# An RWKV-style block on one core: one list of pieces in place of ranks and a planner, and three activation table sets instead of two

## The chip, the cores and the metric

The kernel runs on one core of one Trainium2 chip. The metric is the device time in microseconds. TensorE (PE) multiplies matrices, VectorE (DVE), ScalarE (ACT) and GpSimd (POOL) work on elements, and SyncE (SP) issues most of the DMAs; each engine works through its own instructions in their order. Everything is float32.

## The reference, cut to what matters

```python
# x: 8 batches of 256 tokens, 512 channels; 32 heads of 16
xn = ln(x); sx = token_shift(xn) - xn                    # the token before
xxx = tanh((xn + sx * maa_x) @ maa_w1)                   # five groups of 32
x5 = xn + sx * (maa_stack + xxx @ maa_w2)                # five mixed inputs
w = exp(-exp(time_decay + tanh(x5[1] @ decay_w1) @ decay_w2))
r, k, v = x5[3] @ Wr.T, x5[0] @ Wk.T, x5[2] @ Wv.T
g = silu(x5[4] @ Wg.T)
for t in range(256):                                     # a scan over the tokens
    a = k[t] * v[t];  out[t] = r[t] @ (u * a + s);  s = a + w[t] * s
x = x + (groupnorm(out) * gn_w + gn_b) * g @ Wo.T
xn2 = ln(x); xk, xr = xn2 + sx2 * ffn_maa_k, xn2 + sx2 * ffn_maa_r
x = x + sigmoid(xr @ Wr2.T) * (relu(xk @ Wk2.T) ** 2 @ Wv2.T)
```

## The kernel before, in words

The kernel first describes its work as 2679 pieces (`Op`): 394 on PE, 498 on DVE, 1136 on ACT, 379 on POOL and 272 DMAs on SP's queue. A piece is one instruction, or on PE a group of matmuls that go together. Only then are the pieces put in order and emitted; within an engine that order is the order of the instructions.

The pieces come in three stages for each of the 8 batches `b`. `inputs_of_scan` takes the layer norm (`normed`, `ahead`), transposes (`psT`, L633), makes `xin`, multiplies it by `maa_w1` (`psx`), takes the tanh (`ta`), mixes (`psm`, five groups `x5_b_g`, on DVE L803 or L799 and POOL L809), multiplies by the decay weights (`psd`, then the tanh `tb` and `w`) and projects to k, r, v and g (`psk`, `psr`, `psv`, `psg`; L438). `scan` multiplies r by k (`pc`), and for each of four blocks of channels fills `wrep` with the decay on ACT (L955; there is one buffer `wrep`, in PSUM), loads v broadcast over the partitions (`vs`), multiplies by k (DVE L972), scans (DVE L974, into `st8`), multiplies by r (POOL L977) and gathers on PE (`pat`, L985). `rest` takes the group norm (`sq`, `pv`, `rs`; the copies in L1040 spread `rs` over the partitions into `rsb`), multiplies by `Wo` (`pso`), and runs the feed-forward part (`psfk`, `psfr`, `psfv`). PSUM has six buffers `ps` for all of PE's results.

Batch 0 begins with its own input `xt0`, the vectors `vec`, the identity `idt`, and the centering matrix `cen`, by which PE multiplies the raw weights `Wraw0` and `Wraw1` (`psW`). `xw` are four small products of `vec` on DVE (L567) that batch 0's `xin` needs. Twelve matmuls on zeros come ahead of all that.

In the kernel before, each piece has a rank (`TURNS`, a row for each stage). `order` is a planner: it takes the pieces by rank, gives each a start from costs and delays written in the kernel (`LATENCY`, `LANDS`, `TAKES`), gives it a buffer of its pool that is planned to be free (the one freed latest), and sorts by planned start. A matmul also reserves the tile that its result will be copied into (`into`).

A matmul's weights are loaded either as 128 columns or as four tiles of 32 columns; `tiles` chooses per piece by what stands ahead of it on PE.

ScalarE's functions need a table set to be loaded. `Exp` and `Ln` use one set, `Tanh` and `Silu` another; where the next piece needs the other one, a load is emitted (L1132).

Of the kernel before, what the change touches and what calls it, by code (L numbers as in the profile page):

```python
# [12 lines left out]
P = 128  # L13
# [11 lines left out]
TABLES = {"tanh": "silu_and_others", "exp": "natural_log_exp_and_others"}  # L25
# [15 lines left out]
class Buf:  # L41


    def __init__(self, pool, name, view=lambda t: t):
        self.pool, self.name, self.place, self.left, self.view = pool, name, None, 0, view
        self.writers, self.readers, self.until = [], [], 0.0
        self.before, self.since = set(), 0.0
# [15 lines left out]
class Op:  # L63
    def __init__(self, engine, us, outs, ins, emit, mode):
        self.engine, self.us, self.emit, self.mode, self.narrow = engine, us, emit, mode, False
        self.bufs = list(dict.fromkeys([*outs, *ins]))
        self.before, self.after, self.waits = [], [], 0
        self.ready = self.start = self.end = 0.0
        self.number, self.kind = 0, engine + "".join(c for c in self.bufs[0].name if not c.isdigit())


class Plan:
# [4 lines left out]
    LATENCY = {"PE": 0.25, "DVE": 0.13, "ACT": 0.14, "POOL": 0.06, "DMA": 1.65}  # L77
    LANDS = {"vs__": (2.44, 1.6), "s": (0.1, 1.7), "vo_": (0.4, 1.9), "vo__": (0.46, 1.5), "o_": (0.4, 1.6), "ms": (0.15, 2.0), "rb": (0.9, 1.8), "xn__": (0.8, 1.7), "x": (2.3, 1.1), "xt": (1.65, 2.1), "xt_": (0.8, 1.7),
             "Wo_": (1.75, 1.5), "Wfk_": (1.7, 1.5), "Wfr_": (1.75, 1.4), "Wfv_": (1.65, 1.5), "Wg": (1.6, 2.4), "y_": (0.3, 0.6)}
    EARLY = {"xt0_0": (0.76, 1.28), "xt0_1": (0.76, 1.2), "cen": (0.35, 2.1), "vec": (0.2, 2.3), "xt1": (1.4, 2.3), "xt2": (1.4, 2.0), "idt": (0.17, 2.4), "Wfr0_1": (1.4, 1.5),  # L80
             "Wraw0": (1.65, 2.1), "Wraw1": (1.65, 2.0)}
    SWITCH = {"ACT": 1.38, "PE": 0.11}
    AHEAD = {"PE": 0.1}
    GAP = {"PE": 0.0, "DVE": 0.16, "ACT": 0.12, "POOL": 0.12, "DMA": 0.03}

    TAKES = {("ACTsq_", 0.315): 0.415, ("ACTrsb_", 0.315): 0.415, ("ACTpsm__", 0.405): 0.358, ("ACTxn__", 0.495): 0.45, ("ACTw_", 0.405): 0.357,
             ("ACTw_", 0.315): 0.33, ("ACTtb", 0.315): 0.39, ("ACTta", 0.315): 0.28, ("ACTk_", 0.53): 0.48, ("ACTr_", 0.53): 0.48, ("ACTv_", 0.53): 0.485,
             ("ACTg_", 0.53): 0.494, ("ACTo_", 0.53): 0.495, ("ACTxn__", 0.102): 0.085, ("ACTmn_", 0.102): 0.11, ("ACTatt_", 0.394): 0.374, ("ACTvs__", 0.193): 0.19,
             ("ACTvo_", 0.37): 0.4, ("ACTsq_", 0.405): 0.49, ("PEpsm__", 0.875): 0.945, ("PEpsm__", 0.45): 0.52, ("PEpsw_", 0.875): 0.915, ("POOLvs__", 1.959): 2.25}
    LOOSE = ("ACTatt_", "ACTrsb_", "ACTsq_", "ACTxn__", "ACTxk_", "ACTxr_", "ACTxin_", "ACTxh__", "ACTtb", "ACTw_", "ACTold_")  # L90
    SMALL = ("ACTsq_", "ACTrsb_", "ACTatt_")

    def __init__(self):
        self.stages, self.pools, self.bufs = [[]], {}, {}

    def pool(self, name, tiles):
        self.pools[name] = [[0.0, t] for t in tiles]
        self.bufs[name] = []
# [6 lines left out]
    def add(self, engine, us, outs, ins, emit, mode=None, into=(), lag=0.0, kb=0, part=False):  # L105
        outs, ins, into = ([getattr(b, "buf", b) for b in bs] for bs in (outs, ins, into))
        op = Op(engine, us, outs, ins, emit, mode)
        op.lag, op.wire = self.LATENCY[engine] + lag, 0.0
        op.small = 0.12 if op.kind in self.SMALL and round(us, 3) in (0.315, 0.394) else 0.0
        op.shared = engine == "DVE" and (op.kind in ("DVEhm", "DVExk_") or op.bufs[0].name.startswith("x5_0_2") and round(us, 3) == 0.603)  # L110
        op.gap = 0.0 if op.kind in self.LOOSE else self.GAP[engine]
        op.us = self.TAKES.get((op.kind, round(us, 3)), us)
        if kb:
            name = op.bufs[0].name
            op.wire, op.lag = self.EARLY.get(name) or self.LANDS.get("".join(c for c in name if not c.isdigit()), (kb / 370, 2.0))


        op.bufs += [b for b in into if b not in op.bufs]
# [10 lines left out]
        for o in edges - {op}:  # L129
            op.before.append(o)  # L130
            o.after.append(op)
        self.stages[-1].append(op)

    def stage(self):

        self.stages.append([])
        return len(self.stages) - 2


    TURNS = """  # L140
# [236 lines left out]
def tile_rwkv_block(  # L377
# [25 lines left out]
    nc = tc.nc  # L403
# [805 lines left out]
```

## Time and profile before

| | |
|---|---|
| median of 3 runs | 605.47 us (604.45 to 605.61) |
| profiled execution, its span (first to last instruction) | 604.9 us |
| PE busy | 593.1 us (98%) |
| DVE busy | 538.8 us (89%) |
| ACT busy | 516.8 us (85%) |
| POOL busy | 507.9 us (84%) |
| table loads by the planner's order (L1132) | 43, 1283 ns each |
| moved by DMA | 128.07 MB, mean 212 GB/s |

The profiled execution's own time is its span and what lies around it; it isn't listed beside the runs, and the span lies between their lowest and highest time. A line number belongs to the kernel before. Many lines are those of helpers: L438 is every ordinary matmul, L427 every DMA on SP. "Idle before" is the time in which an engine stood still ahead of an instruction, with what ended it.

### The profile page before, as it was taken

The page shows a single profiled execution, that of the slowest core. Times are in us where ns is not written, and L with a number is a line of the kernel's source. Part 1 is how long each engine was busy: PE and PEld are TensorE (multiplying, and loading weights), DVE is VectorE, ACT ScalarE, POOL GpSimd, SP SyncE. Part 2 cuts the span into 40 slices and gives each one's busy share as a digit, 9 for nine tenths or more (in the row PEclk, how much of TensorE's full clock was granted, in tenths as well). Part 3 has the DMA queues.
Part 4 walks back from the last instruction along what each step waited for, and adds up shares of the span by engine and source line. Part 5 has one row for each costly group of instructions (what it writes and reads, how often), then busy time and mean ns, then how long its engine had stood idle before and what let it go on. Part 6 is the DMA issues. An engine that isn't in the chain of part 4 may idle for free.

```text
span 604.9 us, 19630 instructions
## 1 busy us (share of the span) xinstructions
PE 593.1 (98%) x8236; PEld 345.0 (57%) x8236; DVE 538.8 (89%) x500; ACT 516.8 (85%) x1207; POOL 507.9 (84%) x390
## 2 busy tenths in 40 slices
PE   8899999899999999999999999999999999999997
PEld 7675656467438864365553754465654474455464
DVE  5699999999999999998789999999999999994432
ACT  4898989999999999988999898999999889964531
POOL 0689999989999998999979899999989998996030
PEclk8999999999999999999999999999999999999999
DMA  8895967598988888879666999779776977954341
GB/s 291 267 232 134 244 188 200 152 254 215 240 217 234 231 239 230 242 222 253 151 192 176 260 244 269 193 192 268 207 209 213 273 194 199 283 164 138 124 174 58
DMA packets 55497, 128.07 MB, mean 212 GB/s; under 512 B 6112, under 2 KB 13680, under 8 KB 55408
## 3 DMA queue, kind: packets, MB, share of 16 engines
q1 hardware_dynamic: 51040, 122.61, 74.0%
q10 hardware_dynamic: 4368, 4.20, 2.1%
q8 instruction: 65, 1.06, 0.8%
q14 instruction: 24, 0.20, 0.1%
HBM read 118.39 MB, written 8.40 MB: 210 GB/s over the span
## 4 chain that ended last, share of the span: by engine, by line
PE 88%; ACT 8%; DVE 1%; DMA 1%; issue 1%; SPq 0%; POOL 0%
PE ps L438 75%; PE ps L985 9%; PE ps L849 2%; PE ps L633 2%; ACT ps L797 1%; DMA Ws<-in_consts 1%; ACT L1132 1%; PE ps L1011 1%; ACT sq L1040 1%; ACT rk L1040 1%; PE ps L927 0%; ACT xh L617 0%; ACT att L935 0%; SPq L427 0%; ACT vs L965 0%
## 5 line engine op out<-in xcount | busy, mean ns | idle before, releaser
L974 DVE TENSOR_TENSOR_SCAN st<-wrep,vs 128x1024 f32<-128x1024 f32 x128 | 288.9, 2278 | 3.4 <-ACT wrep L955 1.9
L977 POOL TENSOR_TENSOR st<-st,r 128x1024 f32<-128x1024 f32 x128 | 254.2, 2001 | 11.7 <-DVE st L974 9.1
L972 DVE TENSOR_TENSOR vs<-vs,ps 128x1024 f32<-128x1024 f32 x125 | 147.4, 1208 | 3.0 <-ACT ps L953 2.5
L438 PE MATMUL ps<-Ws,mix 128*32 128x512 f32 (+3 forms) x836 | 115.4, 585 | 0.0
L438 PEld LDWEIGHTS ps<-Ws,mix 128*32 128x32 f32 (+1 forms) x836 | 38.2, 118 | 62.4 <-issue 54.4
L809 POOL TENSOR_TENSOR mix<-mix,xn 128x512 f32<-128x512 f32 x62 | 66.4, 1091 | 3.9 <-DVE mix L799 2.7
L985 PE MATMUL ps<-st,con 128*32 128x256 f32 x1024 | 61.8, 380 | 0.0
L438 PE MATMUL ps<-mix,Wv 128*32 128x256 f32 (+1 forms) x808 | 60.1, 380 | 1.0 <-DVE mix L803 1.0
L438 PE MATMUL ps<-mix,Wr 128*32 128x256 f32 (+1 forms) x832 | 60.4, 380 | 0.4 <-ACT w L855 0.2
L438 PE MATMUL ps<-mix,Wk 128*32 128x256 f32 (+1 forms) x880 | 59.3, 379 | 0.0
L438 PE MATMUL ps<-mix,Wg 128*32 128x256 f32 (+1 forms) x808 | 58.9, 379 | 0.0
L438 PE MATMUL ps<-mix,Ws 128*32 128x256 f32 (+1 forms) x928 | 57.7, 379 | 0.0
L438 PE MATMUL ps<-Ws,g 128*32 128x512 f32 (+1 forms) x464 | 57.0, 593 | 0.4 <-issue 0.4
L1132 ACT ACT_TABLE_LOAD x43 | 55.2, 1283 | 1.2 <-ACT v L880 0.4
L677 POOL TENSOR_TENSOR mix<-mix,xn 128x512 f32<-128x512 f32 x44 | 47.6, 1099 | 6.7 <-ACT mix L675 5.6
L438 PEld LDWEIGHTS ps<-mix,Wv 128*32 128x32 f32 (+1 forms) x808 | 39.0, 117 | 19.1 <-issue 1.4
L438 PEld LDWEIGHTS ps<-mix,Wr 128*32 128x32 f32 (+1 forms) x832 | 39.4, 116 | 17.6 <-issue 2.6
L438 PEld LDWEIGHTS ps<-mix,Wk 128*32 128x32 f32 (+1 forms) x880 | 39.4, 114 | 16.9 <-issue 0.8
L935 ACT COPY att<-ps 32x256 f32<-32x256 f32 x128 | 46.6, 364 | 2.8 <-PE ps L927 1.0
L438 PEld LDWEIGHTS ps<-mix,Wg 128*32 128x32 f32 (+1 forms) x808 | 37.8, 117 | 17.8 <-issue 1.1
L985 PEld LDWEIGHTS ps<-st,con 128*32 128x32 f32 x1024 | 34.3, 110 | 23.4 <-issue 2.5
L438 PEld LDWEIGHTS ps<-mix,Ws 128*32 128x32 f32 (+1 forms) x928 | 34.9, 113 | 21.7 <-issue 1.3
(134 smaller groups left out, 944.5 us busy)
## 6 DMA issues: line engine op xcount, KB each, us to landing
vs<-vo SPq DMA_DIRECT2D x128, 512.0 KB, 5.7
Ws<-in_fk SPq DMA_DIRECT2D x16, 512.0 KB, 5.9
Ws<-in_wo SPq DMA_DIRECT2D x16, 512.0 KB, 6.2
Ws<-in_fr SPq DMA_DIRECT2D x16, 512.0 KB, 7.8
Ws<-in_fv SPq DMA_DIRECT2D x16, 512.0 KB, 4.7
x<-in_x SPq DMA_DIRECT2D x11, 512.0 KB, 6.3
vo<-v ACTq DMA_DIRECT2D x15, 256.0 KB, 3.9
out<-o SPq DMA_DIRECT2D x15, 256.0 KB, 2.5
```

What stands on the lines that cost most here:

```text
L438: nc.tensor.matmul(out[i : i + n], lhsT=w[:, i : i + n], rhs=x, start=first, stop=final)
L633: nc.tensor.transpose(ps()[:, m, n * P : (n + 1) * P], xh[n]()[:, k * P : (k + 1) * P], idt())
L677: gp(512, t, [t, xn[q]], lambda q=q, t=t: nc.gpsimd.tensor_tensor(t(), t(), xn[q]()[:, :, 1 : T + 1], ALU.add))
L809: gp(512, t, [t, xn[q]], lambda q=q, t=t: nc.gpsimd.tensor_tensor(t(), t(), xn[q]()[:, :, 1 : T + 1], ALU.add))
L849: nc.tensor.matmul(pd()[i : i + 32, 0, :], lhsT=w, rhs=src[k // 2]()[:, k % 2, :], start=(k == begin), stop=(k == end))
L935: act(350, atts[q], [pc], lambda i=32 * (2 * q + m), m=m, q=q, h=32 * h: nc.scalar.copy(atts[q]()[h : h + 32, m, :], pc()[i : i + 32, 0, :]))
L972: dve(4 * T, [vs], [vs, kp], lambda m=m, vs=vs, kp=kp: nc.vector.tensor_tensor(vs(), vs(), kp()[:, m : m + 1, :].to_broadcast([P, 4, T]), ...
L974: dve(4 * T, [st], [w, vs], lambda w=w, vs=vs, st=st: nc.vector.tensor_tensor_scan(st().rearrange("p n t -> p (n t)"), w().rearrange("p n ...
L977: gp(4 * T, st, [st, r], lambda m=m, st=st, r=r: nc.gpsimd.tensor_tensor(st(), st(), r()[:, m : m + 1, :].to_broadcast([P, 4, T]), ALU.mul ...
L985: nc.tensor.matmul(pat()[32 * i : 32 * i + 32, 0, :], lhsT=con()[:, s : s + 32], rhs=done[i]()[:, j, :], start=(j == 0), stop=(j == 3),)
L1040: act(256, rsb, [rs], lambda blk=2 * q + n, n=n, rows=rows, rsb=rsb: nc.scalar.copy(by_block(rsb)[rows, n, :], rs()[32 * blk : 32 * blk + ...
L1132: nc.scalar.preload_act_table_set(TABLES[table])
```

## The change

The ranks, the planner and its costs go. In their place stands one list, `ORDER`, with the numbers of all 2679 pieces in the order in which they are emitted. The pieces themselves are the same. A piece takes, of the free buffers of its pool, the one whose last user stands earliest in the list. `into` goes.

The table sets are now three, with Exp and Tanh together in one of them: `{ln, exp}`, `{exp, tanh}`, `{tanh, silu}`. Where the set that is loaded doesn't have the next function, `tables` takes the set that serves the longest run of pieces ahead. By the lists this makes 33 loads.

```diff
-TABLES = {"tanh": "silu_and_others", "exp": "natural_log_exp_and_others"}
+TABLES = {"natural_log_exp_and_others": {"ln", "exp"}, "exp_and_others": {"exp", "tanh"}, "silu_and_others": {"tanh", "silu"}}
+FIRST = "natural_log_exp_and_others"
...
-    TURNS = """
...
+    ORDER = """
+        37 38 2 0 23 39 40 41 42 43 44 45 14 15 46 16 17 22 47 57 34 25 28 31 363 48 49 58 53 59 50 54 60 55 364 366
...
-    def order(self, phases):
-        self.sequence(phases)
...
-                    b.slot = max((s for s in self.pools[b.pool] if s[0] <= at), key=lambda s: s[0])
...
-        done.sort(key=lambda op: op.start)
+    def order(self):
+
+        numbers = [int(n) for n in self.ORDER.split()]
+        assert sorted(numbers) == list(range(len(self.ops)))
+        done = [self.ops[n] for n in numbers]
+        for n, op in enumerate(done):
             for b in op.bufs:
                 if b.place is None:
...
+                    slots = self.pools[b.pool]
+                    slot = min((s for s in slots if s[0] is not None), key=lambda s: s[0])
+                    b.slot, b.place = slots.index(slot), slot[1]
+                    slots[b.slot] = (None, slot[1])
             for b in op.bufs:
                 b.left -= 1
                 if b.pool and not b.left:
+                    self.pools[b.pool][b.slot] = (n, b.place)
         self.tiles([op for op in done if op.engine == "PE"])
+        self.tables([op for op in done if op.engine == "ACT" and op.mode])
         return done
...
+    def tables(self, ops):
+
+        runs = dict.fromkeys(TABLES, 0)
+        best = [None] * len(ops)
+        for n in reversed(range(len(ops))):
+            runs = {t: runs[t] + 1 if ops[n].mode in TABLES[t] else 0 for t in TABLES}
+            best[n] = max(TABLES, key=lambda t: runs[t])
+        now = FIRST
+        for op, table in zip(ops, best):
+            if op.mode not in TABLES[now]:
+                now = op.table = table
...
-            rs(), mv()[:, :, 1], AF.Ln, bias=eh(), scale=over), "exp", 1)
+            rs(), mv()[:, :, 1], AF.Ln, bias=eh(), scale=over), "ln", 1)
...
-            if op.engine == "ACT" and op.mode and op.mode != table:
-                table = op.mode
-                nc.scalar.preload_act_table_set(TABLES[table])
+            if op.table:
+                nc.scalar.preload_act_table_set(op.table)
```

The first pieces on SP's queue, before: `xt0_0 xt0_1 idt xt1 vec Wraw0 cen Wraw1 mw1 mw2a`; after: `xt0_0 xt0_1 vec idt Wraw0 cen xt1 Wraw1 mw1 mw2a`. On PE behind `pv0`, before: `psg1_0 pc1 psk2_1 psv2_0 psv2_0 psd2 psk2_1 psr2_0 psr2_0 psm2_4`; after: `psk2_1 psd2 psv2_0 psg1_0 psr2_0 psk2_1 psv2_0 psr2_0 psm2_4 pc1`.

More of the change, by code (lines that the diff above doesn't have):

```diff
@@ L45, in __init__ @@
         self.pool, self.name, self.place, self.left, self.view = pool, name, None, 0, view
-        self.writers, self.readers, self.until = [], [], 0.0
-        self.before, self.since = set(), 0.0
+        self.writers, self.readers, self.before = [], [], set()
     def __call__(self):
@@ L64, in __init__ @@
     def __init__(self, engine, us, outs, ins, emit, mode):
-        self.engine, self.us, self.emit, self.mode, self.narrow = engine, us, emit, mode, False
+        self.engine, self.us, self.emit, self.mode, self.narrow, self.table = engine, us, emit, mode, False, None
         self.bufs = list(dict.fromkeys([*outs, *ins]))
-        self.before, self.after, self.waits = [], [], 0
-        self.ready = self.start = self.end = 0.0
-        self.number, self.kind = 0, engine + "".join(c for c in self.bufs[0].name if not c.isdigit())
+        self.before, self.wire = [], 0
@@ L72 @@
 class Plan:
[L77 to L89, printed above, removed]
@@ L103, in fixed, with add @@
         return b
-    def add(self, engine, us, outs, ins, emit, mode=None, into=(), lag=0.0, kb=0, part=False):
-        outs, ins, into = ([getattr(b, "buf", b) for b in bs] for bs in (outs, ins, into))
+    def add(self, engine, us, outs, ins, emit, mode=None, kb=0, part=False):
+        outs, ins = ([getattr(b, "buf", b) for b in bs] for bs in (outs, ins))
         op = Op(engine, us, outs, ins, emit, mode)
[L108 to L118, printed above, removed]
+        op.wire = kb
         edges = set()
@@ L128, in add @@
             b.writers.append(op)
[L129 to L137, printed above, removed]
-    TURNS = """
[125 rows of a table removed]
-    """
-    def sequence(self, phases):
-        rows = iter(self.TURNS.split(","))
-        turns = {0: next(rows)}
-        for kind in range(3):
-            for p in range(NB):
-                turns[next(i for k, i in phases[p + kind] if k == kind and i)] = next(rows)
-        self.ops = []
-        for i, turn in turns.items():
-            lot, turn = self.stages[i], turn.split()
-            assert len(turn) == len(lot)
-            for op, t in zip(lot, turn):
-                op.rank = int(t)
-            self.ops += lot
-        for op in self.ops:
-            for b in op.bufs:
-                b.left += 1
@@ L285, in order @@
-    def order(self, phases):
-        self.sequence(phases)
-        free = dict.fromkeys(self.LATENCY, 0.0)
-        free["PE"] = 5.0
-        mode, done, queue, put_off, wire, issue, lanes = dict.fromkeys(free), [], [], [], 0.0, 0.0, [0.0] * 8
-        mode["ACT"], small, self.crossed, began = "exp", 0.0, 0.0, 0.0
-        for n, op in enumerate(self.ops):
-            op.number, op.waits = n, len(op.before)
-            if not op.waits:
-                heapq.heappush(queue, (op.rank, n))
-        while queue:
-            op = self.ops[heapq.heappop(queue)[1]]
-            at = max([free[op.engine], op.ready] + [b.since for b in op.bufs])
-            need = {}
+        op.before = [o for o in self.ops if o in edges]
@@ L299, in order @@
+        for b in op.bufs:
+            b.left += 1
+        self.ops.append(op)
+    def order(self):
[3 more added lines that the diff above has]
+        for n, op in enumerate(done):
             for b in op.bufs:
                 if b.place is None:
-                    need[b.pool] = need.get(b.pool, 0) + 1
-            ahead = self.AHEAD.get(op.engine, 0.0)
-            at = max([at] + [sorted(s[0] for s in self.pools[p])[n - 1] + ahead for p, n in need.items()])
@@ L304, in order @@
-            if at == float("inf"):
-                put_off.append(op)
-                continue
-            if op.wire:
-                if op.engine == "DMA":
-                    at = max(at, lanes.pop(0))
-                    self.crossed += max(0.0, issue - at)
-                else:
-                    issue = max(at, issue)
-            want, now = op.mode, mode[op.engine]
-            if op.engine == "PE":
-                if want == "any":
-                    want = "any" if now in (None, "rows32", "rows64") else now
-                elif now == "any" and want in ("columns", "turn"):
-                    mode["PE"] = now = want
@@ L319, in order @@
-            if want and want != now:
-                if now is not None or op.engine != "PE":
-                    at = max(at, free[op.engine] + self.SWITCH[op.engine])
-                mode[op.engine] = want
-            for b in op.bufs:
-                if b.place is None:
-                    b.slot = max((s for s in self.pools[b.pool] if s[0] <= at), key=lambda s: s[0])
-                    b.since, b.slot[0], b.place = b.slot[0], float("inf"), b.slot[1]
-            if op.engine == "ACT":
-                if op.small and not small:
-                    at = max(at, free["ACT"] + op.small)
-                small = op.small
@@ L331, in order @@
-            op.start, op.end = at, at + op.us
-            if op.shared and began < op.end:
-                op.end = max(op.end, free["POOL"] + 0.28)
-            if op.engine == "POOL":
-                began = at
-            if op.engine == "PE" and at > free["PE"] + 2:
-                op.end += 1.6
-            free[op.engine] = landed = op.end
-            if op.wire:
-                landed = wire = max(wire, op.start + 1.0) + op.wire
-                if op.engine == "DMA":
-                    lanes.append(landed + op.lag)
+                    slots = self.pools[b.pool]
@@ L351, in order @@
-            for o in op.after:
-                same = o.engine == op.engine and not op.wire
-                o.ready = max(o.ready, op.end + op.gap if same else landed + op.lag + self.AHEAD.get(o.engine, 0.0))
-                o.waits -= 1
-                if not o.waits:
-                    heapq.heappush(queue, (o.rank, o.number))
-            done.append(op)
-        if len(done) < len(self.ops):
-            raise RuntimeError("no piece of work can start: too few buffers")
-        self.span = max(op.end for op in done)
@@ L877, in projected @@
                 t = got[what, q] = new(what, f"{what}{b}_{q}")
[L878 removed]
+                ps = project(pieces(W[what]), x5[g], q, f"ps{what}{b}_{q}")
                 lo = int(what == "v")
```

81 lines of the change are left out of this document (34 added, 47 removed), and 240 rows, old and new, of tables (ORDER, TURNS).

## The prediction

> **What bounds the kernel now.** I read the page first, then the busy time by stretch, then the order of time on single engines at the places where the stretches lose something.
>
> ```profile
> span 604.9 us, 19630 instructions
> PE 593.1 (98%) x8236; PEld 345.0 (57%) x8236; DVE 538.8 (89%) x500; ACT 516.8 (85%) x1207; POOL 507.9 (84%) x390
> L1132 ACT ACT_TABLE_LOAD x43 | 55.2, 1283 | 1.2 <-ACT v L880 0.4
> ```
>
> ```profile
> 0.00:21.01 21.01, 16.50 (x145) 14.93 (x145) 11.72 (x34) 12.05 (x28) 2.77 (x14) 0.92 0.93 313
> 21.01:103.00 81.99, 81.80 (x1396) 52.62 (x1400) 77.93 (x80) 72.76 (x163) 76.50 (x57) 1.00 0.78 199
> 103.00:118.83 15.83, 13.71 (x253) 7.85 (x246) 15.78 (x11) 15.52 (x35) 14.99 (x11) 1.00 0.52 151
> 118.83:240.00 121.17, 121.17 (x1698) 74.63 (x1706) 120.21 (x97) 116.79 (x292) 113.93 (x86) 1.00 0.88 233
> 240.00:270.00 30.00, 29.83 (x437) 13.86 (x440) 28.49 (x27) 27.87 (x73) 28.45 (x24) 1.00 0.84 239
> 270.00:345.00 75.00, 74.90 (x1147) 40.96 (x1140) 66.21 (x57) 69.05 (x167) 67.29 (x52) 1.00 0.76 202
> 345.00:540.00 195.00, 195.00 (x2748) 106.51 (x2748) 191.63 (x164) 177.71 (x408) 183.97 (x136) 1.00 0.81 221
> 540.00:600.37 60.37, 60.21 (x440) 33.65 (x438) 26.23 (x35) 25.11 (x46) 20.02 (x16) 1.00 0.42 146
> 600.37:604.90 4.53, 0.00 (x0) 0.00 (x0) 0.58 (x2) 0.00 (x0) 0.00 (x0) 0.82 0.21 62
> ```
>
> The columns are length, then busy time of PE, PEld, DVE, ACT and POOL. TensorE (PE) is the bound: 593.1 of 604.9 us. A new order removes no matmul, so it can win only what PE loses: 4.51 us idle in the first 21.01, and 2.74 us from there to its last matmul (0.19 + 2.12 + 0 + 0.17 + 0.10 + 0 + 0.16). The 4.53 us behind the last matmul is the last additions and the stores. VectorE comes close behind: in 118.83 to 240 it is idle for 0.96 us of 121, in 345 to 540 for 3.4 of 195, but in 240 to 345 for 10.3 of 105.
>
> **The change, part by part.** The 2679 pieces are the same. Counted in the two lists: on PE 203 of 394 pieces keep their place and none moves by more than 11 places; ScalarE's order moves most (573 of 1136 pieces out of sequence). PE changes its kind of tile 73 times before and 72 times after. Such a change costs about 0.13 us, from the same gathering of 32 matmuls with and without one ahead of it:
>
> ```profile
> 146.41 1.86 PE ps L985 x32
> 177.40 1.73 PE ps L985 x32
> ```
>
> One fewer: -0.1 us.
>
> *Buffers.* A piece now takes, of the free buffers of its pool, the one whose last user stands earliest in the list, and a matmul no longer reserves the tile that its result is copied into. No instruction comes or goes with that, so it costs nothing by itself; if a buffer comes free late, that is a new wait, priced below.
>
> *Table loads.* With three sets, the new order needs 33 loads where the old one has 43. Ten loads of 1.28 us are 12.8 us of ScalarE. ScalarE is off the bound for nearly the whole span, so they are costed at nothing by themselves; what covers them is PE's own 593 us. They count only where ScalarE makes PE wait, below.
>
> *The start.* Five DMAs are reordered on SP's queue: `vec` goes from fifth to third, `idt` from third to fourth, `Wraw0` from sixth to fifth, `cen` from seventh to sixth, and `xt1` from fourth to seventh, behind `cen`. On VectorE the four small `xw` products (L567) move ahead of batch 1's statistics. On PE the first half of `psd0` moves ahead of `psv0_0`.
>
> ```profile
> 1.65 0.42 SPq L427 DMA_DIRECT2D idt<-in_consts  x1
> 2.59 0.47 SPq L427 DMA_DIRECT2D vec<-in_vecs  x1
> vec<-in_vecs SPq DMA_DIRECT2D x1, 64.0 KB, 5.0
> 6.80 1.09 PE L633 MATMUL ps<-idt,xh 128*128 128x128 f32 x8 [0.51 <-DVE xh L607]
> 9.29 4.54 PE L438 MATMUL ps<-Ws,Ws 128*128 128x128 f32 x24 [1.40 <-DMA Ws<-in_consts]
> 10.00:11.00 1.00, 1.00 (x7) 1.00 (x6) 0.90 (x3) 0.70 (x4) 0.00 (x0) 0.50 1.11 373
> 13.67 1.89 PE L438 MATMUL ps<-mix,mw 128*128 128x256 f32 x8
> 18.99 1.06 PE L633 MATMUL ps<-idt,xh 128*128 128x128 f32 x8 [0.59 <-DVE mix L803]
> 21.01 3.72 PE L438 MATMUL ps<-mix,Wv 128*128 128x256 f32 x16 [0.96 <-DVE mix L803]
> 9.32 0.30 ACT L575 ACTIVATE rs<-mv,few 128x2 f32<-128x2 f32 x1 [1.03 <-DVE few L567]
> 9.52 0.55 ACT L640 ACTIVATE mix<-ps,vec,few 128x256 f32<-128x256 f32 x1
> 14.52 1.28 ACT L1132 ACT_TABLE_LOAD   x1
> 15.81 0.38 ACT L774 ACTIVATE ta<-ps 128x256 f32<-128x256 f32 x1
> 17.57 2.05 DVE L803 SCALAR_TENSOR_TENSOR mix<-ps,vec,sx 128x256 f32<-128x256 f32 x5 [2.54 <-PE ps L438]
> 18.92 1.09 POOL L809 TENSOR_TENSOR mix<-mix,xn 128x512 f32<-128x512 f32 x1 [0.87 <-DVE mix L803]
> ```
>
> `xin0` (L640) starts at 9.52, and ScalarE was idle before it until `xw` was there (`few` is its tile). `vec` issued at 1.65 lands at about 6.65 with the 5.0 us of its row. Two `xw` products now stand ahead of the second `xh`, which may hold the transposes from 6.80 to about 7.45, and `xin0` can then start near 8.3: 1.2 us earlier. All that follows hangs on it: `psx0` (13.67), the table load, `ta` (15.81), and VectorE's mixing (17.57). With `psd0` first, PE starts its unbroken work after four mixes of 0.41 (2.05 / 5) and one addition on POOL (1.09), so 2.8 us after the mixing starts, plus 0.2 of hand-over: 17.57 - 1.2 + 3.0 = 19.4, where now it starts at 21.01. That is -1.6 us. The bounds: 0, if `ta` hangs on something that hasn't moved (`mw` is issued at the same place in the queue), and -3.2, if the 1.40 us wait for `cen` and the half clock behind it also turn into progress. I take -1.6, the path worked out from rows.
>
> The clock: the granted clock is 0.50 in the row 10 to 11, behind two idle stretches of 0.51 and 1.40 us. If the new list leaves PE idle between the `W` products and `psx0`, `psx0` at half clock takes up to 1.89 us more (its row at 13.67, doubled), which eats the whole term: that is its end 0. The Trainium skill's page "TensorE: Matmul & The Clock Gate", section "Part 1: The HAM clock gate", has the clock fall only after an idle window of about 3.4 us. The trace does not agree (1.40 us was the longest gap). By the page nothing would be lost to the clock in either start, and the term would stay at -1.6.
>
> *ScalarE's chain behind `pv0`.* This is the one large wait, in the row 103 to 118.83. These are pieces of the chain of waits, and PE's row where it ends:
>
> ```profile
> 99.01 0.57 PE ps L1011 x8
> 103.90 0.49 ACT vs L965 x2
> 107.73 1.28 ACT L1132
> 111.58 1.28 ACT L1132
> 112.88 1.03 ACT wrep L955
> 113.91 1.01 ACT att L1046 x2
> 114.92 0.47 ACT v L880
> 115.39 0.49 ACT k L880
> ```
>
> ```profile
> 115.92 0.69 PE L438 MATMUL ps<-tb,mw2b 32*64 32x256 f32 x16 [1.54 <-ACT k L880]
> ```
>
> From the end of `pv0` (99.58) ScalarE works without a gap to 115.88, 16.3 us; then the copy of `k` frees the PSUM buffer that `psm2_4` waits for. PE has less to do meanwhile and loses 2.12 us (1.54 of it just ahead of 115.92). In the new list both table loads and all 16 copies (L1040) still stand in this chain, but `psm2_4` waits for the copy of `r`, which has ahead of it two `vs` fewer (0.49), one `att` fewer (0.51) and one copy fewer (0.47): 14.8 us. PE's work from `pv0` to `psm2_4` is eight halves of a projection, at the 1.73 us of a gathering with as many matmul passes: 13.8 us. About 1.0 of the 2.12 us stays: -1.1 us, between 0 and -2.1.
>
> *The rest.* Of the other 0.62 us of idle, 0.16 stands in the last 60 us, whose PE order is nearly the same; I take -0.3 of the rest. Where matmuls are only spaced wider the busy rows hide it; I put that, as an estimate, at the size of the known rest: -0.6, between 0 and -2. New waits: the list before was also worked out ahead of time, and met 2.74 us of waits on the chip. The new one meets the same at most twice over; I take +0.7, since the cause of the largest one (ScalarE) has 12.8 us less to do, with 0 and +5.5 as ends.
>
> Sum: -0.1 - 1.6 - 1.1 - 0.3 - 0.6 + 0.7 = -3.0 us. The profiled span of 604.9 becomes 601.9. The median shown, 605.47, lies 0.57 above that span (the runs go from 604.45 to 605.61, around it), so the time is **602.5**.
>
> **The rivals.**
> *The gains are given back.* The waits move from the places above to others, and only the start's -1.6 and +1.6 of new waits are left: 605.5, no change (within 0.2%, 1.2 us, which is about what a measurement of this kernel can tell). For it: PE's 0.00 idle in 118.83 to 240 and 345 to 540 with three other engines above 90%; any slip there is new. Against it: ScalarE's 12.8 us.
> *VectorE becomes the bound, and the time is slower.* `wrep` is one buffer: each of its 32 fills on ScalarE (1.03 us, the row at 112.88) comes between VectorE's scans of two blocks. ScalarE's order is the one that moves most. If a fill is late by 0.25 us on average, VectorE loses 8 us; its idle in 240 to 345 (10.3) can hide what is lost ahead of it, but the 195 us behind hold only 3.4. About half of the fills fall there: 4 us against 3.4, and it decides from there on. At 0.5 us late: 8 - 3.4 = 4.6 us longer, less the gains of 3.0: 607.1. Against it: with fewer loads ScalarE should be earlier, not later, at the fills.
> *More is won:* the start at -3.2, the chain at -2.1, no new waits: -0.1 - 3.2 - 2.1 - 0.6 - 1.0 = -7.0, 598.5.
>
> **How the numbers follow.** Forecast 0.60, given back 0.16, slower 0.14, more won 0.10. Faster: 0.60 + 0.10 and a share of the second: 0.72. Same 0.14, slower 0.14. The range leaves out the last part of the slow and of the fast case: 599.6 to 606.2; the forecast's own range is 600.5 to 604.2.
>
> **What would show it.** Right: 33 loads in the row of table loads; `xin0` (L640) near 8.3; PE unbroken from about 19.4; about 1.0 us idle ahead of the `tb` matmuls near 114; VectorE above 98% from 118 to 240. Wrong: `psx0` still near 13.6, or waits of PE for POOL's `st` or ACT's copies in stretches that now show 0.00 idle.

## The result, and the profile after

The changed kernel takes **612.06 us** (median; 609.47 to 613.81) where the kernel before takes 605.54 beside it: a ratio of 1.0111, interval 1.0085 to 1.0137. The forecast was 602.5 (599.6 to 606.2), faster; the kernel became slower. Lines of the changed kernel are 108 lower than those shown before (L438 is L330, L974 is L866, L985 is L877), a few lines higher or lower in some experiments.

The head of the page, and the table loads of its groups (the profiled execution took 613.81, the longest of the four):

```profile
span 612.0 us, 19636 instructions
PE 596.1 (97%) x8260; PEld 344.9 (56%) x8260; DVE 539.3 (88%) x500; ACT 505.8 (83%) x1197; POOL 508.5 (83%) x390
L1019 ACT ACT_TABLE_LOAD x33 | 42.3, 1283 | 0.6
```

The ten loads are gone, as predicted, and ScalarE (ACT) has 11.0 us less to do. The span is 7.1 us longer all the same. Windows of the changed kernel, cut near those of before, and one single microsecond (length; busy PE, PEld, DVE, ACT, POOL; granted clock, DMA share, GB/s):

```profile
0.00:21.01 21.01, 16.98 (x180) 14.62 (x184) 13.53 (x38) 13.37 (x33) 3.71 (x15) 1.00 0.93 315
21.01:103.00 81.99, 80.27 (x1416) 48.37 (x1411) 76.53 (x76) 67.70 (x157) 76.23 (x57) 1.00 0.77 191
103.00:122.00 19.00, 17.23 (x264) 8.83 (x260) 17.19 (x13) 17.87 (x39) 17.35 (x13) 0.91 0.79 192
122.00:240.00 118.00, 118.00 (x1670) 68.44 (x1666) 116.60 (x94) 111.40 (x277) 110.14 (x83) 1.00 0.87 229
240.00:285.00 45.00, 43.33 (x578) 22.71 (x574) 38.94 (x39) 39.56 (x98) 40.60 (x33) 1.00 0.83 219
285.00:345.00 60.00, 59.61 (x942) 33.32 (x936) 53.93 (x44) 55.94 (x137) 52.44 (x43) 1.00 0.76 209
345.00:418.00 73.00, 72.78 (x1127) 42.92 (x1123) 70.10 (x59) 63.43 (x157) 69.54 (x53) 1.00 0.81 219
418.00:427.00 9.00, 6.44 (x114) 3.54 (x110) 4.86 (x6) 6.48 (x19) 8.70 (x7) 1.00 0.90 223
427.00:540.00 113.00, 112.87 (x1564) 62.94 (x1564) 112.05 (x89) 97.50 (x223) 99.38 (x73) 1.00 0.83 220
...
608.74:612.00 3.26, 0.00 (x0) 0.00 (x0) 0.58 (x2) 0.00 (x0) 0.00 (x0) 1.00 0.26 80
118.00:119.00 1.00, 1.00 (x16) 0.57 (x12) 1.00 (x2) 1.00 (x4) 0.64 (x1) 0.50 0.97 217
```

Read the idle of TensorE (PE) as length less busy. Up to the last matmul at 608.74 it is 608.74 - 596.1 = 12.6 us, where the kernel before has 600.37 - 593.1 = 7.3. The start lost less (4.03 against 4.51 us). New idle stands where the list before had nearly none: 1.72 us from 21 to 103 (0.19 before), 1.67 from 240 to 285, 2.56 from 418 to 427 (0.00 before from 345 to 540). PE's busy time is 3.0 us longer too, and the end behind the last matmul 1.3 us shorter (3.26 against 4.53): 5.3 + 3.0 - 1.3 gives the 7 us.

What PE, ScalarE and the SP queue waited for in the two kernels, by lines of their tables of waits and of DMA issues (us in total, times, longest; KB each and median us from issue to landing). First the changed kernel:

```profile
PE ps L877 <- DVE mix L724: 2.6, 1, 2.6
ACT vs L857 <- DMA vs<-vo: 9.8, 8, 2.7
SPq L319 <- DMA vo<-v: 73.3, 9, 10.5
vo<-v ACTq DMA_DIRECT2D x15, 256.0 KB, 5.5
```

Then the kernel before:

```profile
SPq L427 <- DMA vo<-v: 22.8, 4, 7.3
vo<-v ACTq DMA_DIRECT2D x15, 256.0 KB, 3.9
```

`v` goes out to memory (`vo<-v`) and comes back as the rows of the scan (`vs<-vo`). ScalarE stood still eight times for such rows, 9.8 us in all. The largest new stall of PE can be followed in the timeline of the changed kernel (start, length, what, and in brackets the idle before it with its releaser):

```profile
407.80 0.58 SPq L319 DMA_DIRECT2D Ws<-in_fk  x1
409.70 0.37 ACTq L841 DMA_DIRECT2D vo<-v  x1
417.84 1.16 SPq L319 DMA_DIRECT2D vs<-vo  x2
419.97 0.38 ACT L747 ACTIVATE w<-ps 64x256 f32<-64x256 f32 x1
421.20 1.93 PE L330 MATMUL ps<-mix,Wv 128*32 128x256 f32 x32
422.81 0.30 ACT L857 ACTIVATE vs<-s,cm 128x4 f32<-128x4 f32 x1 [2.46 <-DMA vs<-vo]
424.66 1.16 ACT L722 ACTIVATE ps<-ps,vec 128x256 f32<-128x256 f32 x3
425.69 1.67 PE L877 MATMUL ps<-st,con 128*32 128x256 f32 x25 [2.56 <-DVE mix L724]
```

A weight load goes out at 407.80 and `v`'s write (`vo6_0`) at 409.70. SP waits for the write with nothing else issued until 417.84, then loads the rows. ScalarE has come to the piece that needs them (`vs6_1_3`) at 420.35 and stands for 2.46 us. Behind that piece are the reads of PSUM (L722) that VectorE's mixing needs, and PE's next product waits for the PSUM buffer that the mixing frees. The names in the wait, VectorE and its mixing, are the last link only. Paired with the list in order, SP's issues and ScalarE's pieces show how little time the order leaves: the load of `vs6_1_3` is issued at 417.84 and ScalarE comes to its piece 2.5 us later; in the kernel before, the load goes out at 423.97 and the piece starts at 436.06, 12.1 us later, without a wait.

### The profile page after: what moved, and what is told of

The parts are those of the page before. It is cut to its first block, busy times and chain, and to the rows that moved or that the text cites. A ratio compares the mean times of both kernels' runs of the same rounds, so it can differ in the third digit from the quotient of the medians.

```text
span 612.0 us, 19636 instructions
## 1 busy us (share of the span) xinstructions
PE 596.1 (97%) x8260; PEld 344.9 (56%) x8260; DVE 539.3 (88%) x500; ACT 505.8 (83%) x1197; POOL 508.5 (83%) x390
## 4 chain that ended last, share of the span: by engine, by line
PE 78%; ACT 7%; DMA 6%; POOL 4%; DVE 3%; issue 1%; SPq 1%; ACTq 0%; DVEq 0%; POOLq 0%
PE ps L330 66%; PE ps L877 8%; DMA vs<-vo 3%; DMA Ws<-in_fk 2%; PE ps L525 1%; PE ps L741 1%; POOL mix L701 1%; ACT ps L689 1%; DMA sq<-ms 1%; POOL st L869 1%; ACT att L827 1%; DVE mix L695 1%; ACT L1019 1%; DVE st L493 1%; SPq L319 1%
## 5 line engine op out<-in xcount | busy, mean ns | idle before, releaser
L866 DVE TENSOR_TENSOR_SCAN st<-wrep,vs 128x1024 f32<-128x1024 f32 x128 | 288.9, 2278 | 6.9 <-ACT wrep L847 3.9
L330 PE MATMUL ps<-Ws,mix 128*32 128x512 f32 (+3 forms) x836 | 117.3, 585 | 0.5 <-ACT o L967 0.4
L330 PEld LDWEIGHTS ps<-Ws,mix 128*32 128x32 f32 (+1 forms) x836 | 41.0, 118 | 59.5 <-issue 48.3
L877 PE MATMUL ps<-st,con 128*32 128x256 f32 x1024 | 63.7, 385 | 3.6 <-DVE mix L724 2.6
L330 PE MATMUL ps<-mix,Wr 128*32 128x256 f32 (+1 forms) x736 | 61.7, 380 | 0.6 <-issue 0.4
L330 PE MATMUL ps<-mix,Wg 128*32 128x256 f32 (+1 forms) x784 | 61.0, 379 | 0.6 <-issue 0.6
L330 PE MATMUL ps<-mix,Wv 128*32 128x256 f32 (+1 forms) x904 | 60.3, 380 | 0.3 <-DVE mix L695 0.3
L330 PE MATMUL ps<-mix,Wk 128*32 128x256 f32 (+1 forms) x928 | 59.9, 380 | 0.3 <-POOL mix L701 0.3
L330 PE MATMUL ps<-mix,Ws 128*32 128x256 f32 (+1 forms) x928 | 58.5, 379 | 0.2 <-DMA Ws<-in_fk 0.2
L330 PE MATMUL ps<-Ws,g 128*32 128x512 f32 (+1 forms) x464 | 57.6, 598 | 0.0
L330 PEld LDWEIGHTS ps<-mix,Wr 128*32 128x32 f32 (+1 forms) x736 | 40.8, 120 | 16.9 <-issue 3.1
L877 PEld LDWEIGHTS ps<-st,con 128*32 128x32 f32 x1024 | 34.5, 111 | 27.9 <-POOL att L833 3.0
L330 PEld LDWEIGHTS ps<-mix,Wg 128*32 128x32 f32 (+1 forms) x784 | 39.6, 118 | 17.7 <-issue 2.0
L330 PEld LDWEIGHTS ps<-mix,Wv 128*32 128x32 f32 (+1 forms) x904 | 37.6, 113 | 20.7 <-issue 3.1
L550 POOL TENSOR_TENSOR sx<-xn 128x512 f32<-128x512 f32 x22 | 22.8, 1045 | 31.6 <-ACT xn L546 31.6
L330 PEld LDWEIGHTS ps<-mix,Ws 128*32 128x32 f32 (+1 forms) x928 | 36.9, 113 | 20.6 <-issue 1.3
L330 PEld LDWEIGHTS ps<-mix,Wk 128*32 128x32 f32 (+1 forms) x928 | 36.1, 113 | 21.5 <-issue 2.6
```

The costliest lines, as they stand in the source:

```text
L330: nc.tensor.matmul(out[i : i + n], lhsT=w[:, i : i + n], rhs=x, start=first, stop=final)
L550: take(512, [sx], [xn], lambda xn=xn, sx=sx, e=nc.vector if alone and q else nc.gpsimd: e.tensor_tensor(sx(), xn()[:, :, 0:T], xn()[:, :, ...
L866: dve(4 * T, [st], [w, vs], lambda w=w, vs=vs, st=st: nc.vector.tensor_tensor_scan(st().rearrange("p n t -> p (n t)"), w().rearrange("p n ...
L877: nc.tensor.matmul(pat()[32 * i : 32 * i + 32, 0, :], lhsT=con()[:, s : s + 32], rhs=done[i]()[:, j, :], start=(j == 0), stop=(j == 3),)
```

## The experiments

All lists below were compared with the kernel before on the same chip, in five rounds. Runs put on record at different times had different chips (e1 to e4, e5 to e8, e9 to e11, e12 to e14), on which the kernel before took 604.65 to 605.59 us; across these groups the ratios compare better than the times. "Old list" is the order of before, "new list" that of the change; pieces have the names of their tiles. The first three theories: T1, ScalarE's pieces stand too early for their loads; T2, the transfers are late by their order; T3, the table sets or the rule for buffers cost the time.

**e1: the old list in the changed code.**

```
-    ORDER = """ 37 38 2 0 23 39 40 ... """
+    ORDER = """ (the order that the planner of before gives) """
```

> The changed kernel's code (its rule for buffers, its three table sets), with the emission order of the kernel before written out as the list. Theory 1 (in the new list ScalarE's in-order queue stands still for `vs` and `rb` loads that land late): the list is the cause, so 604 to 607 us. Theory 2 (the new order of the DMAs makes loads late, and the wait would only move elsewhere): the same, 604 to 607. Theory 3 (the new choice of table sets or the new rule for buffers costs the time): 609 to 613.

Measured: 608.95 us, ratio 1.0055 (1.0038 to 1.0072). About 4 us come with the code, without the new list: just below the range of T3 and above that of T1 and T2. Seen by this run alone it could be the sets or the buffers; e5 and e6 part them.

**e2: the new list, two table sets.**

```
-TABLES = {"natural_log_exp_and_others": ..., "exp_and_others": {"exp", "tanh"}, "silu_and_others": ...}
+TABLES = {"natural_log_exp_and_others": ..., "silu_and_others": ...}
```

> The new list with the two table sets of the kernel before: 49 loads in place of 33, some 20 us more on ScalarE. Theories 1 and 2: slower than the changed kernel, 612 to 620 us, since ScalarE is in the chain of its waits. Theory 3: faster than the changed kernel, below 609.

Measured: 623.13 us, 1.0301 (1.0266 to 1.0337), 49 loads. On the new list, whose order has three sets in mind, the third set is worth 11 us. The time lies above the range of T1 and T2 (612 to 620), and T3 had it below 609.

**e3: seven pieces of ScalarE later (new list).**

```
vs0_1_3 +8, vs1_1_3 +3, vs3_1_3 +5, pb5 +4, vs5_0_1 +12, vs6_1_3 +12, vs6_1_0 +6 places in ScalarE's order
```

> The new list with seven pieces of ScalarE moved later (six `vs` and `pb5`, by 3 to 12 pieces), those at which it stood still for a load; all else as in the new list. Theory 1: the waits of PE behind them go (about 1.4 + 1.7 + 1.7 + 2.6 us), 603 to 607 us. Theory 2: the waits move to VectorE and POOL, which need the same loads: 610 to 613. Theory 3: no change, 610 to 613.

Measured: 613.44 us, 1.0130 (1.0105 to 1.0155): no gain. In its trace the stall at 421 is gone, but PE now stands 1.53 us ahead of 60.69 and 1.85 us ahead of 385.62. The chains behind both lead back to moved pieces that had become late themselves (`vs0_1_3`, and `vs5_0_1`, for which VectorE stood 3.14 us at 369). So this run does not decide on T1; e7 does.

**e4: half of the weights' bytes (new list).**

```
-        load_pairs(tiles, src)
+        if b: (each tile by its first 256 columns only)
+        else: load_pairs(tiles, src)
```

> The changed kernel, with the weights of `Wo` and the feed-forward part loaded for batch 0 whole and for batches 1 to 7 only by their first 256 columns (14.7 of 128 MB less; from batch 1 on the output isn't the reference's). Theories 1 and 2: `vo` and `vs` land earlier, ScalarE's waits for loads shrink from 9.8 us to less than half, 604 to 608 us. Theory 3: no change, 610 to 613.

Measured: 606.16 us, 1.0018 (1.0001 to 1.0034). 14.7 MB less take 5.9 us off, `v`'s write lands in 4.4 us instead of 5.5, and ScalarE stands still for the rows for 3.6 us instead of 9.8. The output isn't the reference's. The transfers matter (T2); e12 has the control.

**e5 and e6: sets and buffers apart, on the old list.** e5 has the new rule for buffers and two sets; e6 has three sets and the places of before.

```
e5:  -"exp_and_others": {"exp", "tanh"},
e6:  -  slot = min((s for s in slots if s[0] is not None), key=lambda s: s[0])
     +  slot = slots[int(next(take))]        (the places of before, written out)
```

> The old list and the new rule for buffers, with two table sets as before (43 loads where the old list with three sets has 37). The old list under the changed code took 608.95 us; in its trace four loads moved to stand directly ahead of an ln (sq3_0 at 297, rn7 at 370, sq4_0 at 385, rs2_4 at 422), and each set ScalarE back by 1.3 to 1.5 us. If the table sets cost that time: 604.9 to 606.0 us, and the stalls of TensorE at 304 and 310 (0.50 and 0.89), 383 (1.04) and 422 (0.44 and 0.50) are gone. If the new rule for buffers costs it: 608 to 609.5 us with those stalls.

> The old list and the three table sets, each buffer in the place that the planner of before gave it (a written list of places takes the place of the rule). If the table sets cost the 4 us of the old list under the changed code: 608 to 609.5 us, with the four loads ahead of ln. If the rule for buffers costs them: 604.9 to 606 us. If each costs a part, this run and the one with two sets lie between, and their losses over 605 us add up to about 4 us.

Measured: e5 605.24 us, 0.9990 (0.9973 to 1.0006); e6 608.51 us, 1.0046 (1.0028 to 1.0063). The rule for buffers costs nothing. The three sets cost the old list 3 to 4 us although they save it six loads. The reason stands in the timelines. e1, three sets:

```profile
382.39 0.64 PE L905 MATMUL ps<-sq,con 128*32 128x256 f32 x8
383.79 1.28 ACT L1021 ACT_TABLE_LOAD   x1
385.08 0.47 ACT L910 ACTIVATE sq<-ps,few 128x256 f32<-128x256 f32 x1
385.61 1.92 PE L332 MATMUL ps<-Ws,mix 128*32 128x512 f32 x16 [0.86 <-ACT sq L910]
```

e5, two sets, the same place:

```profile
381.70 0.80 ACT L691 ACTIVATE ps<-ps,vec 128x256 f32<-128x256 f32 x2
382.41 0.48 ACT L910 ACTIVATE sq<-ps,few 128x256 f32<-128x256 f32 x1
382.93 0.42 ACT L912 ACTIVATE sq<-sq 128x256 f32<-128x256 f32 x1
```

With two sets the set with `ln` and `exp` had been loaded ahead of an `exp` piece (`wrep5_1`) two microseconds earlier, and the `ln` (L910) found its table. With three, that `exp` went with the `tanh` set, and the load now stands directly ahead of the `ln` that reads PSUM, with PE waiting for that very buffer. A load is saved where ScalarE had time, and one is put where it has none. The place alone doesn't decide: the changed kernel too has a load directly ahead of the `ln` of `sq3_0`, `sq4_0` and `rs2_4` (300.4, 386.8 and 428.9), and its PE shows no wait behind them.

**e7: only two of the seven moves (new list).**

```
vs6_1_3 +14, pb5 +4 places in ScalarE's order
```

> The new list with only two pieces of ScalarE moved later: vs6_1_3 (behind which ScalarE stood still for 2.46 us at 420.4) by 14 places, pb5 (1.84 us at 279.6) by 4. Seven moves at once gained nothing (613.44 us), but in that trace the stall of TensorE at 421.2 (2.77 us) was gone and that at 280.5 was down from 1.12 to 0.63, while new ones stood at 57 (1.72) and 382 (2.03) where two other pieces had been moved. If a late load under an in-order ScalarE is what these two stalls are: 608.5 to 609.8 us (612.06 less 2.8 and 0.5). If every stall only comes back elsewhere: 611.3 to 613 us.

Measured: 608.47 us, 1.0048 (1.0029 to 1.0066), so 3.6 us less than the changed kernel. ScalarE's waits for the rows shrink with it (waits of e7; its profiled execution is the shortest of its runs):

```profile
ACT vs L859 <- DMA vs<-vo: 3.2, 3, 2.4
```

PE's wait of 2.56 us is gone from that trace, and the one of 0.92 us ahead of 283.34 is down to 0.27. T1 holds for these two places: one small piece, late by its load, held up the whole in-order engine.

**e8: the new start ahead of the old list.** The first 132 pieces of the new list, then the old one, two sets.

```
-    ORDER = """ (old list) """
+    ORDER = """ (new list's first 132 pieces) (the rest in the old list's order) """
```

> The first 132 pieces of the new list (to about 25 us), then the old list, with two table sets and the new rule for buffers. If the start's gain is real and stays (its trace has 0.7 us less lost between 0 and 30 us and a first matmul 0.2 us earlier): 0.9 us under the old list with two sets, 604.0 to 605.1 us. If it is given back at the next place where TensorE waits (the ScalarE chain at 112): the same time as the old list with two sets, within 0.4 us.

Measured: 605.72 us, 1.0001 (0.9987 to 1.0016). The new start gains nothing that lasts. All 12 runs had a mean clock of 0.999 or more, and the 8 runs of e5 with such a clock have a median of 604.46, so at full clock this version is rather slower than e5.

**e9: three reads of PSUM ahead of a table load (old list, near 111 us).**

```
- ... g1_0, (load) wrep1_1, att0_0 x2, v2_0, k2_1, r2_0 ...
+ ... g1_0, v2_0, k2_1, r2_0, (load) wrep1_1, att0_0 x2 ...
```

> The old list with two table sets (605.24 us), and near 111 us three pieces of ScalarE moved ahead of one table load and of wrep1_1: the reads of PSUM v2_0, k2_1 and r2_0, for which TensorE waits at 113.9 (1.72 us) and at 116 and 108 (0.6 and 0.55). wrep1_1, and VectorE's scans behind it, come 1.8 us later. If ScalarE's order ahead of that stall is the price of it and VectorE has room: 603.3 to 604.3 us, the stall at 113.9 under 0.3 us. If VectorE is the bound there and the late fill of wrep1_1 is passed on: 605 to 607 us, with TensorE waiting later for st81 or att1.

Measured: 610.00 us, 1.0093 (1.0072 to 1.0114): worse than either expectation. The stall that the move was to take away went down (1.72 to 0.87 us, counted from the start of the `tb` group to the start of the next, less what its matmuls take), but a larger one opened behind it. Timeline of e9:

```profile
113.52 0.59 ACT L774 COPY r<-ps 128x512 f32<-128x512 f32 x1 [1.91 <-PE ps L332]
114.13 1.28 ACT L1021 ACT_TABLE_LOAD   x1
116.48 4.47 DVE L868 TENSOR_TENSOR_SCAN st<-wrep,vs 128x1024 f32<-128x1024 f32 x2 [3.52 <-ACT wrep L849]
121.37 4.91 PE L332 MATMUL ps<-Ws,g 128*32 128x512 f32 x28 [4.36 <-issue]
```

ScalarE stood 1.91 us for PE ahead of the copy of `r`, with `wrep1_1` and the pieces of `att0` queued behind it. VectorE then stood 3.52 us for `wrep1_1`, and PE 4.36 us ahead of the projection that needs `att0`. On in-order engines a read moved ahead can only move to where its matmul is done.

**e10 and e13: two weight loads later (new list), alone and with e7's moves.**

```
Wfr0_0: from 28.5 us to just ahead of Wfr0_1;  Wfk4_0: from 407.8 us to just ahead of Wfk4_1
```

> The new list with two weight loads moved back to just ahead of their own second halves: Wfr0_0 (issued at 28.5, first needed at 167) and Wfk4_0 (issued at 407.8, first needed at 447). In the changed kernel's trace v's write that is issued behind each landed after 8.2 and 8.0 us, where the kernel before showed 4.4 for the same write, and ScalarE then stood still 2.65 us at 49.4 and 2.46 us at 420.4. If these two loads in front of v's way through memory are the cause: writes landing in 4 to 5.5 us, the stall of TensorE at 421.2 (2.77) gone and those at 49.5 and 53.7 (1.4 together) halved, 608.3 to 609.8 us. If the loads are late for another reason: 611 to 613 us with the writes still at 7 us and more.

> The new list with vs6_1_3 and pb5 moved later on ScalarE (608.47 us by itself) and with Wfr0_0 and Wfk4_0 loaded later (608.85 us by itself). If the two are two losses: 605 to 606 us. If they are one loss, late loads of the scan's rows under an in-order ScalarE, taken away once from the side of the wait and once from that of the transfer: 607.3 to 609 us.

Measured: e10 608.85 us, 1.0063 (1.0049 to 1.0077); e13 610.13 us, 1.0092 (1.0072 to 1.0112). Alone, the two loads are worth 3.2 us, as T2 expected. In the profiled execution, the longest of its six, the stall at 421 is gone from the side of the transfer: ScalarE comes to `vs6_1_3` at 420.17 and starts it at 420.20, and PE is busy for 8.97 of the 9 us from 414 to 423. Elsewhere the waits stay: the median write lands in 6.4 us (5.5 in the changed kernel), and ScalarE still stands 7.9 us for rows. With e7's moves the time is outside both expectations, and the gain is 1.9 us by the times and 1.2 by the ratios, less than either alone and hardly clear of noise. So they are not two losses that add up. By how much they are one could not be settled: a moved transfer shifts all that come behind it.

**e11: all moves at once (new list).**

```
e7's moves, e10's moves, and e9's three reads ahead of wrep1_1
```

> The new list with three table sets and all moves at once: vs6_1_3 and pb5 later on ScalarE (608.47 us by themselves), the two weight loads later, and v2_0, k2_1, r2_0 ahead of wrep1_1 near 112 (there pc1 waits 2.0 to 2.6 us behind psm2_4). If each piece holds by itself: 608.5 less 1.0 for the loads (49 to 54 us) less 2.0 for the stall at 113 gives 605 to 606.5 us, no better than the kernel before. If the new list has further stalls that only show as others go: 607 to 609 us.

Measured: 613.61 us, 1.0143 (1.0119 to 1.0167). Its trace has e9's stall (5.1 us behind the product that starts at 114.0), so e9's move costs the new list too: 3 to 4 us beside e13, where the old list lost 5 to 6 beside e5 (by the times and by the ratios). The time is outside both expectations.

**e12: half of the weights' bytes on the old list.** The edit of e4, in e5.

> The old list with two table sets (605.24 us), with the weights of Wo and of the three matrices of the channel mixing loaded by their first 256 columns only from batch 1 on (14.7 MB less; the other columns hold what lay there before). On the new list the same cut took 5.9 us off (612.06 to 606.16). If the new list is the one that suffers from late loads: the old list changes by less than 0.8 us, 604.4 to 605.4 us. If fewer bytes help any list (contention in all transfers): 600 to 602 us.

Measured: 604.28 us, 0.9992 (0.9980 to 1.0004). The same cut that gave the new list 5.9 us gives the old one at most 1.0, and nothing by the ratios (e5 has 0.9990). Here too the output isn't the reference's. Traffic is no general bound; the new list is the one that suffers from it.

**e14: TensorE kept at work in the first 10 us (old list, two sets).**

```
-WARM = 12
+WARM = 14
...
+                    if k == 0 and half == 0: (twelve empty matmuls into the buffer of psW0)
```

> The old list with two table sets (605.24 us; 604.46 over its 8 runs with a granted clock of 0.999 or more, 605.47 over the 4 with 0.997), with TensorE kept at work in its first 10 us: two more of the empty matmuls ahead of the program, and twelve ahead of the first product of the W weights, for whose operand it waits 1.5 us. If the idle there sets off the half clock: every run at 0.999 or more, and a median of 604.2 to 604.6 us. If the half clock comes from elsewhere: a third of the runs at 0.997 as before, and 605.0 to 605.5 us. If the empty matmuls hold the real ones up: 605.5 to 606.5 us at full clock.

Measured: 606.41 us, 1.0017 (1.0002 to 1.0031). In the profiled execution no half clock falls on the start, and PE's unbroken work begins earlier than the 21.01 of before:

```profile
20.46 3.72 PE L332 MATMUL ps<-mix,Wv 128*128 128x256 f32 x16 [0.96 <-DVE mix L701]
```

That is where e5 has it too without them (20.42, no half clock either). Ten of the twelve runs had a mean clock of 0.999 or more, where e5 had 8 of 12 and the kernel before, beside this run, 12 of 17; that is too little to show that the idle of the start sets off the drops. In the profiled execution a drop came at 292 us instead, behind waits of 0.79 and 2.14 us. The median, 606.41, lies in the range that was given for empty matmuls that hold the real ones up, but the trace shows none held up at the start, so where this time goes stays open.

## Why the prediction was wrong, step by step

*New waits (+0.7, with ends 0 and +5.5): the term that failed.* It was sized by the waits that the list before had met, on the reason that ScalarE has 12.8 us less to do. The idle that is new by the windows is 1.5 us (21 to 103), 1.8 (240 to 345) and 2.9 (345 to 540): 6.2 us, above its upper end. ScalarE's amount of work was not the question. It stood still 9.8 us for rows that had not landed (no such wait is listed for the kernel before), in an order where they are needed soon after they are asked for. The trace of before showed the queue's waits for `v`'s write (22.8 us), and I priced a wait only on engines, not on SP's queue. e7 and e10 show the mechanism (3.6 and 3.2 us back), e4 with e12 that it belongs to this list.

*Ten fewer loads at nothing.* "They count only where ScalarE makes PE wait" was right as a sentence and not applied: I counted loads and did not look where the remaining ones stand. On the old list six fewer loads cost 3 to 4 us (e6), with four of those left moved to stand directly ahead of an `ln` (one costs PE the 0.86 us shown at 385; that they make up the whole cost was not shown); on the new list the third set is worth 11 us (e2). The sign depends on the list.

*Buffers at nothing.* Right: e5 is within 0.3% of before.

*The start (-1.6).* The path was right: the first piece of `xin0` starts at 7.9 (8.3 was said), and PE's work that was to be unbroken from 19.4 begins at 19.15, where the kernel before has 21.01 and e5 20.42:

```profile
7.89 1.02 ACT L532 ACTIVATE mix<-ps,vec,few 128x256 f32<-128x256 f32 x2 [1.95 <-PE ps L525]
19.15 0.41 PE L741 MATMUL ps<-mix,dw 128*32 128x256 f32 x2 [0.46 <-POOL mix L701]
20.42 3.72 PE L332 MATMUL ps<-mix,Wv 128*128 128x256 f32 x16 [0.95 <-DVE mix L697]
```

The first two lines are the changed kernel's, the third is e5's. But 0.6 of those 1.9 us is the half clock at 9 to 13 in the profile of before: e5, whose profile has none, has that work at 20.42. And the rest is not kept: from 21 to 103 PE loses 1.72 us where it lost 0.19, and e8, which starts the old list so, is no faster than e5 (605.72 against 605.24). The step assumed that all behind the start shifts with PE; that was not so.

*ScalarE's chain behind `pv0` (-1.1).* Mis-sized: PE loses 1.77 us from 103 to 122, where it lost 2.12, so the term measured -0.35. Timeline of the changed kernel:

```profile
113.43 0.80 PE L330 MATMUL ps<-tb,mw2b 32*64 32x256 f32 x12
115.45 0.65 PE L330 MATMUL ps<-tb,mw2b 32*64 32x256 f32 x4 [1.22 <-ACT r L772]
116.52 0.64 PE L819 MATMUL ps<-rk,hm 128*32 128x256 f32 x8 [0.42 <-ACT v L772]
117.29 3.06 PE L877 MATMUL ps<-st,con 128*32 128x256 f32 x32
114.33 4.47 DVE L866 TENSOR_TENSOR_SCAN st<-wrep,vs 128x1024 f32<-128x1024 f32 x2 [0.80 <-ACT wrep L847]
120.46 2.29 DVE L866 TENSOR_TENSOR_SCAN st<-wrep,vs 128x1024 f32<-128x1024 f32 x1 [1.01 <-PE ps L877]
```

`psm2_4` does wait for the copy of `r`, and 1.22 us (about 1.0 was said). But `pc1` (L819) now stands behind it and waits for the copy of `v`, one copy later in ScalarE's order. I named `pc1`'s move and priced only `psm2_4`. VectorE, which had 0.05 us idle between its pieces from 112 to 125 before, now loses 0.80 and 1.01 us there. And the half clock, 1.7 us in the kernel before at 9 to 13, now falls on 118 to 121: the product at 117.29 takes 3.06 us, and 1.93 in the same view of the kernel before (at 116.54).

*Hidden spacing (-0.6).* PE's busy time grew by 3.0 us. With the half clock costing the same in both, this is wider spacing inside the groups, and it was not traced to single places.

*Tile kinds (-0.1) and the rest of the idle (-0.3)* are too small to be told apart from these losses.

*The rivals.* None was it. "VectorE becomes the bound through late fills of `wrep`" has the right side and comes nearest in time (607.1); its mechanism shows: VectorE's scans wait 3.9 us in all for `wrep`, 1.9 before.

```profile
L866 DVE TENSOR_TENSOR_SCAN st<-wrep,vs 128x1024 f32<-128x1024 f32 x128 | 288.9, 2278 | 6.9 <-ACT wrep L847 3.9
L974 DVE TENSOR_TENSOR_SCAN st<-wrep,vs 128x1024 f32<-128x1024 f32 x128 | 288.9, 2278 | 3.4 <-ACT wrep L955 1.9
DVE vs L864 <- ACT vs L857: 5.1, 6, 1.8
```

The second line is the kernel before. By the third, from the changed kernel's waits, VectorE also stood 5.1 us for ScalarE's `vs` pieces (0.4 before): the late rows reach VectorE as well. But PE's longest waits do not come from the fills. "The gains are given back" has the right mechanism, new waits elsewhere, at a fifth of their size.

*What stays open:* about 3 us of the changed kernel's loss, between e7 (608.47) and the kernel before. In e7's profiled execution PE's idle up to its last matmul is 600.60 - 593.4 = 7.2 us, as in the kernel before (7.3, against 12.6 in the changed kernel), and its clock is full to there. So in this execution the new idle is gone in sum, also at places far from the two moves, and what is left is PE's busy time: 593.4 without a half clock, where the kernel before has 593.1 with one that costs 1.7. Which places are spaced wider was not traced, and that execution is the shortest of e7's twelve. No version tried is clearly faster than the kernel before: e5, e8 and e14, and e4 and e12, which load less, are within 0.3% of it.

## What to carry to other kernels

On in-order engines look, for each piece that waits on a transfer, at the time from issue to need, and at what is queued behind the waiting piece: a 0.3 us piece that is 2.5 us late cost the matrix engine 2.6. Count table loads by place, not by number: a rule that saves loads can put the rest ahead of the piece that everything waits for. And a gain at the start is worth nothing until it is shown that the next chain on another engine shifts with it.

## What the runs showed of the hardware

The granted clock of TensorE drops for a fixed time. In every profile where it dropped ahead of the last matmul, it stood at 0.50 for about 3.4 us, which is 1.7 us of full clock: before at 9 to 13, changed kernel at 118 to 121, e9 at 122 to 125, e14 at 292 to 295, and seven more of the experiments (e2 twice). The idle ahead is no sure sign. In the kernel before a wait of 1.54 us ahead of 115.92 was not followed by a drop, and in the changed kernel neither was the longest one, 2.56 us ahead of 425.69; waits of 1.22 and 0.42 us were. The Trainium skill's page "TensorE: Matmul & The Clock Gate", section "Part 1: The HAM clock gate", has a window of 3413 ns that runs freely, without regard to where the kernel stands in it. The traces agree: in their clock records each stretch between two changes lasts a whole number of 3.413 us (in the changed kernel 33 at full clock, one at half, 144 at full; in the kernel before one at full, one at half, 173 at full). A free-running window could also explain why the same order drops in some runs only: the 12 runs of e5 have a mean clock of 0.999 or more in 8 (median 604.46 us) and 0.997 in 4 (605.47). The prediction's reading, that the page's idle window of about 3.4 us does not agree with the trace, holds: the changed kernel's drop came behind no wait longer than 1.22 us. What does set a drop off stays open.
